# A two-layer graph network on one core: statistics, weight sums, exponentials and adds of the first and last groups in other places

## The chip, the cores and the metric

The kernel runs on one core of a Trainium2 chip. A core has five engines that run side by side: PE (TensorE, matrix products), DVE (VectorE, elementwise work and reductions), ACT (ScalarE, activations and copies), POOL (GpSimd, elementwise work on SBUF) and SP (SyncE, here only a queue for DMA issues). Each engine takes its own instructions strictly in program order and waits on semaphores for the others. The metric is the device time of one execution in microseconds (us).

## The reference

The input x is 128 samples of 128 nodes with 512 features, all float32, and adj a 128 x 128 adjacency matrix. There are two layers, each of the form "normalise, cut at zero, mix, add to x":

```python
h = relu(layernorm(x))                       # layer 0
q, k, v = h @ Wq0.T, h @ Wk0.T, h @ Wv0.T
rel = adj.T * (q @ k.T)                      # per sample, 128 x 128
rel = rel / norm(rel, axis=2)
x = x + rel @ v
h = relu(layernorm(x))                       # layer 1, 8 heads of 64
q, k, v = h @ Wq1 + bq, h @ Wk1 + bk, h @ Wv1 + bv
scores = q @ k.T / 8 + where(adj == 0, -1e9, 0)
x = x + concat_heads(softmax(scores) @ v)
```

## The kernel before

**Groups.** Four samples make a group (G = 4), so there are 32 groups. For every group there is an object of layer 0 and one of layer 1. At any time the kernel has several groups in work: in the order lists, `p` is the group whose layer 1 is being finished, `l` the one in layer 1, `m` the one in layer 0, `n` the layer-1 object of m's group, and `f` the next group, whose input is loaded.

**Products.** A 512 x 512 weight is multiplied with the 512-column activations of a group in the form of Strassen and Winograd with seven half-size products instead of eight. `Product.P1` to `P7` (L244 to L263) are these seven. Each is 8 PE passes of 256 columns (4 matrix instructions, each in two passes). They need sums of quarters of the weight (T1 to T4N, made once by `sums`, L88: four DVE or POOL instructions of 128 x 512) and sums of quarters of the activations (s0 to s3, made per group and layer by `sumA` and `sumB`, L348 and L359: four DVE instructions). Results are gathered with ACT copies (`keep`, L237) and DVE adds (`add`, L241). P6 and P7 and P4 go on in the bank of P1 ("x"), P3 in the bank of P5 ("z"), P2 in one of its own ("y").

**Layer 0.** `stat` (L279) computes mean and variance of a sample on DVE, two instructions; `inv` (L286) makes the reciprocal root and shift on POOL for two samples, four instructions; `hn` (L295) normalises on ACT and sends the result to DRAM, `rd` (L307) issues the reads back on SP, and `T` (L310) finishes the transpose on DVE. For the very first group `hn_pe` and `turn_pe` (L318, L329) transpose on PE instead. Wq0 and Wk0 are folded into one matrix "a" (`weights0`, L117: 16 products into four PSUM banks pa, in the middle of which, after the twelfth, the first half of group 0 is turned). `weights_v0` (L133) turns Wv0 on PE into four banks pwv and makes its sums on POOL. Then `G` is h times a, `R` (L377) the relation, `mask_rel` and `square` (L388, L395) on DVE and ACT, `N` (L399) the norms by a product with ones, `V` the values, and `O`, `xO` (L412, L417) the output and its addition to x.

**Layer 1.** `Q`, `K`, `V` are products; `S` (L438) the scores of one sample into a PSUM tile that exists once; `mk` (L452) adds the mask and takes the negative maxima on DVE; `ex` (L458) is eight exponentials on ACT and a DMA of the result to DRAM; `wr` and `wt` (L470, L473) read it back and transpose it; `A`, `oc`, `rdo`, `ot` (L554 to L579) make the output, turn it through DRAM, scale it and add it to x. The last group has its own ending: `mk_r`, `ex_r`, `tw`, `An`, `fin` (L485 to L528) work without the way through DRAM for its last two samples. `fin` scales on DVE, adds x on POOL, or on DVE for the last sample, and stores by SP.

**Order.** The order of work is written by hand: no scheduler moves anything. Four lists of step names (FIRST, SECOND, ORDER, LAST, L603 to L634) are walked step by step, and each step issues its instructions to its engines, so the order of the names is the order in each engine's queue. FIRST is used for group 0, SECOND for group 1, ORDER for the other thirty, LAST for what is left of layer 1. Before FIRST there is a prologue (L649 to L667): statistics of group 0, loads of group 1 and of layer 1's weights (issued by POOL), normalising of group 0, statistics of group 1, and the weights of layer 0.

**Buffers.** A tile of a pool with n buffers waits until the tile n allocations before it in that pool is no longer read. Of importance here: ps_mm (4 PSUM banks, for all products, pa and pwv), ps_o (2 banks, tag "po"), ps_s (the one score tile), rpool (4 buffers "r": what `keep` copies, a12 and v12 of the weights), and work (2 buffers "o", in the ending).

Of the kernel before, what the change touches and what calls it, by code (L numbers as in the profile page):

```python
# [9 lines left out]
F32 = mybir.dt.float32  # L10
AF = mybir.ActivationFunctionType
ALU = mybir.AluOpType
AX = mybir.AxisListType

P = 128
G = 4
# [5 lines left out]
def kernel(  # L22
# [15 lines left out]
    nc = tc.nc  # L38
# [24 lines left out]
    ps_o = ctx.enter_context(tc.tile_pool(name="ps_o", bufs=2, space=PSUM))  # L63
# [4 lines left out]
    def load(g: int, b: int, queue):  # L68
        xb = xpool.tile([P, D], F32, tag="xb", name=f"xb_{g}_{b}")
        queue.dma_start(xb, x[g * G + b])  # L70
        x_tiles[g, b] = xb


    ident = const.tile([P, P], F32, tag="ident", name="ident")
# [13 lines left out]
    def sums(n: str, w12, eng):  # L88
        c = wc[n]
        eng.tensor_tensor(c[:, T1], w12, c[:, W11], ALU.subtract)  # L90
        eng.tensor_tensor(c[:, T2], c[:, W22], c[:, T1], ALU.subtract)
        eng.tensor_tensor(c[:, T3], c[:, W22], w12, ALU.subtract)
        eng.tensor_tensor(c[:, T4N], c[:, W21], c[:, T2], ALU.subtract)
# [16 lines left out]
    w12 = {}  # L110

    def place(n: str, m: int, ps, w12, copy):

        copy(wc[n][:, W11 if m < 2 else W21, m % 2, :], ps[:, 0:HF])
        copy(w12[:, m, :] if m < 2 else wc[n][:, W22, m % 2, :], ps[:, HF:D])

    def weights0(between):  # L117

        a12 = rpool.tile([P, 2, HF], F32, tag="r", name="a12")
        pa = [ps_mm.tile([P, D], F32, tag="mm", name=f"pa_{m}") for m in range(KD)]  # L120
        for k in range(KD):
            for m in range(KD):
                nc.tensor.matmul(
                    pa[m], lhsT=raw["q"][:, k, ts(m, P)], rhs=raw["k"][:, k, :],
                    start=(k == 0), stop=(k == KD - 1),
                )
            if k == KD - 2:
                between()
        for m in range(KD):
            place("a", m, pa[m], a12, nc.vector.tensor_copy)  # L130
        sums("a", a12, nc.vector)

    def weights_v0():  # L133

        v12 = rpool.tile([P, 2, HF], F32, tag="r", name="v12")
        for m in range(KD):
            pt = ps_mm.tile([P, KD, P], F32, tag="mm", name=f"pwv_{m}")
            for k in range(KD):
                nc.tensor.transpose(pt[:, k, :], raw["v"][:, k, ts(m, P)], ident)
            place("v0", m, pt.rearrange("p k e -> p (k e)"), v12, nc.scalar.copy)  # L140
        sums("v0", v12, nc.gpsimd)
        nc.vector.tensor_scalar(mask, adj_sb, 0.0, NEG, ALU.is_equal, ALU.mult)

    def load1():
        for name, w in (("q", wq1), ("k", wk1), ("v1", wv1)):
            wr = w.rearrange("(k p) d -> p k d", p=P)
            nc.gpsimd.dma_start(
                wc[name][:, W11 : W21 + 1].rearrange("p h k d -> p (h k) d"), wr[:, :, 0:HF]
            )
            nc.gpsimd.dma_start(wc[name][:, W22], wr[:, 2:4, HF:D])  # L150
            w12[name] = wpool.tile([P, 2, HF], F32, tag="wT", name=f"w12_{name}")
            nc.gpsimd.dma_start(w12[name], wr[:, 0:2, HF:D])
        nc.gpsimd.dma_start(bq_sb, bq1.rearrange("(e p) -> p e", p=P))
        nc.gpsimd.dma_start(bk_sb, bk1.rearrange("(e p) -> p e", p=P))
        nc.gpsimd.dma_start(bv_sb, bv1.partition_broadcast(P))

    class Weights1:
        def scale(self):

            SC = HD**-0.5  # L160
            nc.scalar.mul(wc["q"][:, 0:3], wc["q"][:, 0:3], SC)
            nc.scalar.mul(w12["q"], w12["q"], SC)
            nc.scalar.mul(bq_sb, bq_sb, SC)

        def sumq(self):
            sums("q", w12["q"], nc.vector)
# [199 lines left out]
    class Layer0(Layer):  # L366
        n = 0
# [54 lines left out]
    class Layer1(Layer):  # L422
        n = 1
# [104 lines left out]
        def fin(self, b):  # L528
            g, xb = self.g, x_tiles.pop((self.g, b))
            o = work.tile([P, D], F32, tag="o", name=f"o_{g}_{b}")  # L530
            nc.vector.tensor_tensor(
                o.rearrange("p (k r d) -> p k r d", k=NH, r=2),
                self.po.pop(b).rearrange("p (k r d) -> p k r d", k=NH, r=2),
                self.rs.pop(b).rearrange("p (r k) -> p k r", r=2)[:, :, :, None].to_broadcast(
                    [P, NH, 2, HD]
                ),
                ALU.mult,
            )
            (nc.vector if b == G - 1 else nc.gpsimd).tensor_tensor(xb, xb, o, ALU.add)
            nc.sync.dma_start(out[g * G + b], xb)  # L540

        def mkA(self, b):
# [58 lines left out]


    FIRST = """  # L603
        m.sumA m.sumB m.start m.G.P1 f.hn0 f.rd0 m.G.P2 m.G.P5 w.scale m.G.P6 w.sumq m.G.P3 m.V.P1 f.hn1 f.rd1
        w.sumv m.G.P7 m.V.P2 w.sumk m.G.P4 m.V.P5
        m.R m.mask_rel m.square f.T0 m.V.P6 m.V.P3 m.N m.norms m.V.P7 m.O0 m.xO0 m.O1 m.xO1 n.stat0 n.stat1
        n.inv0 m.V.P4 n.hn0 n.rd0 f.T1 m.O2 m.O3 f.sumA f.start f.G.P1 m.xO2 m.xO3 n.stat2 n.stat3 n.inv1
        f.G.P2 f.sumB f.G.P5 n.hn1 n.rd1 f.G.P6 f.G.P3 f.G.P7 n.T0 f.G.P4 n.T1 n.start
    """.split()
    SECOND = """  # L610
# [17 lines left out]
    """.split()  # L628
    LAST = """
        l.Q.P1 p.rdo0 l.sumA l.Q.P2 l.sumB l.K.P1 l.K.P2 p.wt3 l.Q.P5 p.ot0 l.Q.P6 l.Q.P3 l.K.P5 l.K.P6 l.K.P3  # L630
        l.Q.P7 l.S0 l.mk0 l.K.P7 l.Q.P4 l.ex0 l.wr0 l.K.P4 l.S1 l.mk1 p.A1 p.oc1 p.rdo1 l.start_v l.V.P1
        l.ex1 l.V.P2 l.V.P5 l.S2 l.mkA2 l.mkB2 l.V.P6 l.exA2 l.exB2 l.wt0 l.wr1 l.V.P3 l.V.P7 l.S3 l.mkA3 l.mkB3
        l.tw2 l.wt1 l.exA3 l.exB3 l.V.P4 l.An0 l.fin0 l.An1 l.fin1 p.ot1 l.tw3 l.An2 l.fin2 l.An3 l.fin3
    """.split()  # L634
# [1 line left out]
    def run(order, **who):  # L636
        for step in order:
            name, *path = step.split(".")
            at = who.get(name)
            if at is None:  # L640
                continue
            if len(path) == 2:
                getattr(getattr(at, path[0]), path[1])()
            elif path[0][-1].isdigit():
                getattr(at, path[0][:-1])(int(path[0][-1]))
            else:
                getattr(at, path[0])()

    with tc.manual_schedule(engines={EN.PE, EN.SP, EN.Pool, EN.DVE, EN.Activation}):  # L649
        p, l, m = None, None, Layer0(0)  # L650
        for b in range(G):
            m.stat(b)
        m.inv(0)
        m.inv(1)
        for b in range(G):
            load(1, b, nc.gpsimd)
        load1()
        m.hn_pe(0)
        m.hn_pe(1)
        f = Layer0(1)  # L660
        for b in range(G):
            f.stat(b)
        f.inv(0)
        f.inv(1)
        weights0(lambda: m.turn_pe(0))
        m.turn_pe(1)
        weights_v0()  # L667
        for g in range(NG):
            n = Layer1(g)
            if g:  # L670
                f = Layer0(g + 1) if g + 1 < NG else None
            run((FIRST, SECOND, ORDER)[min(g, 2)], p=p, l=l, m=m, n=n, f=f, w=Weights1())
            p, l, m = l, n, f
        run(LAST, p=p, l=l)
# [30 lines left out]
```

## Time and profile before

| | us |
|---|---|
| three runs | 2539.89, 2538.28, 2534.71 |
| median | 2538.28 |
| the profiled execution, its own time | 2538.26 |
| its span, first to last instruction | 2536.5 |

| engine | busy us | share of span | instructions |
|---|---|---|---|
| PE | 2512.7 | 99% | 14672 |
| PE weight loads | 2135.8 | 84% | 14672 |
| DVE | 1707.5 | 67% | 2484 |
| ACT | 1023.9 | 40% | 3248 |
| POOL | 535.0 | 21% | 945 |

The mean granted PE clock is 0.997 of full speed. A line in the order of time gives the start and duration in us, the engine, the line of the kernel, the operation, output and inputs with their shapes, how many instructions are merged in it, and in brackets the idle time of the engine before it with what ended that idle time. A line of waits gives who waited for whom, total us, how often, and the longest.

### The profile page before, as it was taken

The page shows a single profiled execution, that of the slowest core. Times are in us where ns is not written, and L with a number is a line of the kernel's source. Part 1 is how long each engine was busy: PE and PEld are TensorE (multiplying, and loading weights), DVE is VectorE, ACT ScalarE, POOL GpSimd, SP SyncE. Part 2 cuts the span into 40 slices and gives each one's busy share as a digit, 9 for nine tenths or more (in the row PEclk, how much of TensorE's full clock was granted, in tenths as well). Part 3 has the DMA queues.
Part 4 walks back from the last instruction along what each step waited for, and adds up shares of the span by engine and source line. Part 5 has one row for each costly group of instructions (what it writes and reads, how often), then busy time and mean ns, then how long its engine had stood idle before and what let it go on. Part 6 is the DMA issues. An engine that isn't in the chain of part 4 may idle for free.

```text
span 2536.5 us, 40820 instructions
## 1 busy us (share of the span) xinstructions
PE 2512.7 (99%) x14672; PEld 2135.8 (84%) x14672; DVE 1707.5 (67%) x2484; ACT 1023.9 (40%) x3248; POOL 535.0 (21%) x945
## 2 busy tenths in 40 slices
PE   8999999999999999999999999999999999999998
PEld 6888888888888888888888888888888888888886
DVE  5566766667676667666677666676666676666765
ACT  2334443444433344434444333444344443334433
POOL 5121212211122212121111222121211112221211
PEclk9999999999999999999999999999999999999999
DMA  5255544555444555445554445554455644455542
GB/s 171 88 179 166 187 145 140 172 170 185 154 145 151 182 167 183 146 146 168 168 188 152 142 155 178 171 182 142 148 169 165 193 151 143 156 176 174 175 133 93
DMA packets 370475, 405.71 MB, mean 160 GB/s; under 512 B 29600, under 2 KB 286752, under 8 KB 370272
## 3 DMA queue, kind: packets, MB, share of 16 engines
q1 hardware_dynamic: 278992, 167.92, 23.4%
q10 hardware_dynamic: 70384, 166.74, 17.8%
q0 software_dynamic: 20896, 68.44, 7.8%
q8 instruction: 115, 1.88, 0.3%
q14 instruction: 88, 0.72, 0.1%
HBM read 204.80 MB, written 198.18 MB: 159 GB/s over the span
## 4 chain that ended last, share of the span: by engine, by line
PE 97%; DVE 1%; DMA 1%; ACT 0%; issue 0%; POOL 0%; SPq 0%; ACTq 0%; DVEq 0%; POOLq 0%
PE pv_x L218 18%; PE pq_x L218 9%; PE pv_z L218 9%; PE pk_x L218 9%; PE pg_x L218 8%; PE pss L445 5%; PE po L562 5%; PE pv_y L218 5%; PE pg_z L218 4%; PE pq_z L218 4%; PE pr L382 4%; PE pk_z L218 4%; PE po L414 4%; PE pk_y L218 2%; PE pg_y L218 2%; PE pq_y L218 2%
## 5 line engine op out<-in xcount | busy, mean ns | idle before, releaser
L463 ACT ACTIVATE e<-pss,nmax 128x128 f32<-128x128 f32 x1008 | 355.0, 380 | 190.9 <-DVE nmax L456 168.5
L597 POOL TENSOR_TENSOR xb<-xb,o 128x512 f32<-128x512 f32 x124 | 158.2, 1276 | 1103.6 <-DVE o L590 976.4
L218 PE MATMUL pv_x<-wc_v,h 128*128 128x256 f32 x1280 | 300.8, 382 | 0.0
L218 PEld LDWEIGHTS pv_x<-wc_v,h 128*128 128x128 f32 x1280 | 240.3, 190 | 51.0 <-DVE v L242 11.7
L301 ACT ACTIVATE hn<-xb,shift,rstd 128x512 f32<-128x512 f32 x252 | 190.9, 807 | 152.4 <-POOL shift L293 152.4
L218 PE MATMUL pv_z<-wc_v,s 128*128 128x256 f32 x1024 | 245.1, 382 | 0.0
L313 DVE STREAM_TRANSPOSE h<-u_h 128x1024 f32<-128x1024 f32 x126 | 156.5, 1242 | 98.9 <-DMA u_h<-d_h 92.0
L463 ACT ACTIVATION_READ_ACCUMULATOR e<-pss,nmax 128x1 f32 x1008 | 221.2, 219 | 0.0
L454 DVE TENSOR_TENSOR pss<-pss,mask 128x1024 f32<-128x1024 f32 x126 | 154.7, 1228 | 96.2 <-PE pss L445 96.2
L218 PEld LDWEIGHTS pv_z<-wc_v,s 128*128 128x128 f32 x1024 | 192.0, 190 | 28.6
L218 PE MATMUL pv_x<-wc_v,s 128*128 128x256 f32 x768 | 184.9, 384 | 0.0
L218 PE MATMUL pq_x<-h,wc_q 128*128 128x256 f32 x768 | 184.7, 383 | 0.0
L283 DVE BATCH_NORM_STATS2 st<-xb 128x6 f32<-128x512 f32 x256 | 172.0, 672 | 16.6 <-DMA xb<-in_x_dram 16.6
L218 PE MATMUL pk_x<-h,wc_k 128*128 128x256 f32 x768 | 181.5, 379 | 0.0
L445 PEld LDWEIGHTS pss<-kT,qT 64*128 64x128 f32 x2048 | 124.6, 188 | 48.7 <-PE po L414 23.5
L290 POOL TENSOR_SCALAR rstd<-mv 128x2 f32<-128x2 f32 x128 | 28.6, 223 | 642.8 <-DVE mv L284 642.7
L218 PEld LDWEIGHTS pq_x<-h,wc_q 128*128 128x128 f32 x768 | 143.4, 190 | 23.5 <-ACT oT L573 5.1
L218 PEld LDWEIGHTS pk_x<-h,wc_k 128*128 128x128 f32 x768 | 145.8, 190 | 19.9
L218 PEld LDWEIGHTS pv_x<-wc_v,s 128*128 128x128 f32 x768 | 140.8, 190 | 20.4
L456 DVE TENSOR_REDUCE nmax<-pss 128x8 f32<-128x1024 f32 x126 | 154.2, 1224 | 4.4
L478 DVE STREAM_TRANSPOSE wT<-u_w 128x1024 f32<-128x1024 f32 x126 | 150.3, 1193 | 3.6 <-DMA u_w<-d_w 3.6
L445 PE MATMUL pss<-kT,qT 64*128 64x128 f32 x2048 | 149.2, 285 | 2.7 <-ACT e L463 2.3
(147 smaller groups left out, 4460.2 us busy)
## 6 DMA issues: line engine op xcount, KB each, us to landing
d_h<-hn ACTq DMA_DIRECT2D x126, 512.0 KB, 3.5
u_h<-d_h SPq DMA_DIRECT2D x504, 128.0 KB, 3.3
d_w<-e ACTq DMA_DIRECT2D x126, 512.0 KB, 2.6
u_w<-d_w SPq DMA_DIRECT2D x504, 128.0 KB, 2.9
xb<-in_x_dram POOLq DMA_DIRECT2D x124, 256.0 KB, 3.2
d_o<-oT ACTq DMA_DIRECT2D x62, 512.0 KB, 4.1
u_o<-d_o SPq DMA_DIRECT2D x248, 128.0 KB, 3.1
out_dram<-xb POOLq DMA_DIRECT2D x124, 256.0 KB, 2.8
```

What stands on the lines that cost most here:

```text
L218: nc.tensor.matmul(ps[:, m, :], lhsT=lhsT, rhs=rhs, start=first and m == 0 and k == 0, stop=k == 1, skip_group_check=True,)
L283: nc.vector.bn_stats(st, x_tiles[g, b])
L301: nc.scalar.activation(hn[:, r], x_tiles[g, b].rearrange("p (k j q) -> p j k q", j=TB, q=BK), AF.Relu, bias=self.shift[:, b : b + 1], scal ...
L313: nc.vector.transpose(half.rearrange("p k (t i) -> p t k i", i=BK), self.u.pop(i).rearrange("p t (k q) -> p t k q", q=BK),)
L382: nc.tensor.matmul(pr[:, b, :], lhsT=self.turned(k, b), rhs=self.gT[:, k, ts(b, P)], start=(k == 0), stop=(k == KD - 1),)
L445: nc.tensor.matmul(pss[:, r, k, :], lhsT=self.qT[rows, k, ts(b, P)], rhs=self.kT[rows, k, ts(b, P)], start=True, stop=True,)
L454: nc.vector.tensor_tensor(sc, sc, mask[:, None, :].to_broadcast([P, H, P]), ALU.add)
L456: nc.vector.tensor_reduce(self.nmax[b], sc, AX.X, ALU.max, negate=True)
L463: nc.scalar.activation(e[:, :, i, :], sc[:, i, :].rearrange("p (j q) -> p j q", q=BK), AF.Exp, bias=nmax[:, i : i + 1], accum_out=self.tot ...
L478: nc.vector.transpose(self.wT[b].rearrange("p h (t i) -> p t h i", i=BK), self.uw.pop(b).rearrange("p t (h q) -> p t h q", q=BK),)
L562: nc.tensor.matmul(po[r * HD : (r + 1) * HD, k, :], lhsT=self.v[:, b, ts(2 * k + r, HD)], rhs=wT[:, r * NH + k, :], start=True, stop=True,)
L597: nc.gpsimd.tensor_tensor(xb, xb, o.rearrange("p k t q -> p (k t q)"), ALU.add)
```

## The change

Six things are done in other places or in another way; the arithmetic is the same.

1. `weights0` allocates a PSUM tile `warm` in ps_o and lets PE transpose the identity into it eight times before its first product. Nobody reads the tile.
2. `stat` of the four samples of group 1 and both `inv` leave the prologue and go into FIRST: statistics 0 and 1 and `inv0` behind the activation sums of group 0, statistics 2 and 3 and `inv1` behind G.P2.
3. The sums of the weight v0 (POOL) leave `weights_v0` and become the step `w.sumw`, behind f.inv1 in FIRST.
4. `w.sumq` (DVE) moves from ahead of G.P3 to behind V.P2, directly ahead of `w.sumk`.
5. Later in FIRST, m.xO2, m.xO3, n.stat2, n.stat3 and n.inv1 go ahead of f.sumA, f.start and f.G.P1.
6. In LAST, the exponentials of sample 0 (`l.ex0`, `l.wr0`) go ahead of l.Q.P4, and the final add of sample 2 is done by DVE instead of POOL.

On PE eight transposes are added at the head and nothing else changes its order. On ACT, G.P5's copy now precedes f.hn0, and in LAST ex0 precedes the copy of Q.P4. On SP the order is the same, on POOL one instruction is gone.

```diff
@@ -117,6 +117,9 @@
     def weights0(between):
 
         a12 = rpool.tile([P, 2, HF], F32, tag="r", name="a12")
+        warm = ps_o.tile([P, P], F32, tag="po", name="warm")
+        for _ in range(8):
+            nc.tensor.transpose(warm, ident, ident)
         pa = [ps_mm.tile([P, D], F32, tag="mm", name=f"pa_{m}") for m in range(KD)]
         for k in range(KD):
             for m in range(KD):
@@ -138,7 +141,7 @@
             for k in range(KD):
                 nc.tensor.transpose(pt[:, k, :], raw["v"][:, k, ts(m, P)], ident)
             place("v0", m, pt.rearrange("p k e -> p (k e)"), v12, nc.scalar.copy)
-        sums("v0", v12, nc.gpsimd)
+        w12["v0"] = v12
         nc.vector.tensor_scalar(mask, adj_sb, 0.0, NEG, ALU.is_equal, ALU.mult)
 
     def load1():
@@ -161,6 +164,9 @@
             nc.scalar.mul(wc["q"][:, 0:3], wc["q"][:, 0:3], SC)
             nc.scalar.mul(w12["q"], w12["q"], SC)
             nc.scalar.mul(bq_sb, bq_sb, SC)
+
+        def sumw(self):
+            sums("v0", w12["v0"], nc.gpsimd)
 
         def sumq(self):
             sums("q", w12["q"], nc.vector)
@@ -536,7 +542,7 @@
                 ),
                 ALU.mult,
             )
-            (nc.vector if b == G - 1 else nc.gpsimd).tensor_tensor(xb, xb, o, ALU.add)
+            (nc.vector if b >= G - 2 else nc.gpsimd).tensor_tensor(xb, xb, o, ALU.add)
             nc.sync.dma_start(out[g * G + b], xb)
 
         def mkA(self, b):
@@ -601,10 +607,10 @@
 
 
     FIRST = """
-        m.sumA m.sumB m.start m.G.P1 f.hn0 f.rd0 m.G.P2 m.G.P5 w.scale m.G.P6 w.sumq m.G.P3 m.V.P1 f.hn1 f.rd1
-        w.sumv m.G.P7 m.V.P2 w.sumk m.G.P4 m.V.P5
+        m.sumA m.sumB m.start f.stat0 f.stat1 f.inv0 m.G.P1 m.G.P2 f.stat2 f.stat3 f.inv1 w.sumw m.G.P5 f.hn0 f.rd0 m.G.P6
+        w.scale m.G.P3 m.V.P1 f.hn1 f.rd1 w.sumv m.G.P7 m.V.P2 w.sumq w.sumk m.G.P4 m.V.P5
         m.R m.mask_rel m.square f.T0 m.V.P6 m.V.P3 m.N m.norms m.V.P7 m.O0 m.xO0 m.O1 m.xO1 n.stat0 n.stat1
-        n.inv0 m.V.P4 n.hn0 n.rd0 f.T1 m.O2 m.O3 f.sumA f.start f.G.P1 m.xO2 m.xO3 n.stat2 n.stat3 n.inv1
+        n.inv0 m.V.P4 n.hn0 n.rd0 f.T1 m.O2 m.xO2 m.O3 m.xO3 n.stat2 n.stat3 n.inv1 f.sumA f.start f.G.P1
         f.G.P2 f.sumB f.G.P5 n.hn1 n.rd1 f.G.P6 f.G.P3 f.G.P7 n.T0 f.G.P4 n.T1 n.start
     """.split()
     SECOND = """
@@ -628,7 +634,7 @@
     """.split()
     LAST = """
         l.Q.P1 p.rdo0 l.sumA l.Q.P2 l.sumB l.K.P1 l.K.P2 p.wt3 l.Q.P5 p.ot0 l.Q.P6 l.Q.P3 l.K.P5 l.K.P6 l.K.P3
-        l.Q.P7 l.S0 l.mk0 l.K.P7 l.Q.P4 l.ex0 l.wr0 l.K.P4 l.S1 l.mk1 p.A1 p.oc1 p.rdo1 l.start_v l.V.P1
+        l.Q.P7 l.S0 l.mk0 l.K.P7 l.ex0 l.wr0 l.Q.P4 l.K.P4 l.S1 l.mk1 p.A1 p.oc1 p.rdo1 l.start_v l.V.P1
         l.ex1 l.V.P2 l.V.P5 l.S2 l.mkA2 l.mkB2 l.V.P6 l.exA2 l.exB2 l.wt0 l.wr1 l.V.P3 l.V.P7 l.S3 l.mkA3 l.mkB3
         l.tw2 l.wt1 l.exA3 l.exB3 l.V.P4 l.An0 l.fin0 l.An1 l.fin1 p.ot1 l.tw3 l.An2 l.fin2 l.An3 l.fin3
     """.split()
@@ -658,10 +664,6 @@
         m.hn_pe(0)
         m.hn_pe(1)
         f = Layer0(1)
-        for b in range(G):
-            f.stat(b)
-        f.inv(0)
-        f.inv(1)
         weights0(lambda: m.turn_pe(0))
         m.turn_pe(1)
         weights_v0()
```

## The prediction

> **What bounds the kernel now.** I read the page's busy shares first, then TensorE's waits over the whole span, then the order of time in the places that these waits name.
>
> ```profile
> PE 2512.7 (99%) x14672; PEld 2135.8 (84%) x14672; DVE 1707.5 (67%) x2484; ACT 1023.9 (40%) x3248; POOL 535.0 (21%) x945
> ...
> PE pa L123 <- DMA raw_q<-in_L_gnn_Wq_dram: 4.6, 1, 4.6
> PE pwv L139 <- issue: 2.5, 1, 2.5
> PE pss L445 <- ACT e L463: 2.3, 2, 2.0
> PE pg_x L218 <- DVE gT L242: 2.0, 2, 1.2
> PE pq_z L218 <- DVE qT L242: 1.0, 1, 1.0
> ```
>
> TensorE (PE) is busy 99% of 2536.5 us. Asked for 140 to 2480 us alone, its waits are none: thirty groups run with no gap, so what the first groups gain reaches the end undiminished, and only the head and the tail can change the time. All waits together are about 14 us, and the five rows above hold most of them. Now the head, in order of time (start, duration, engine, line; what it idled for is in brackets):
>
> ```profile
> 22.75 0.69 DVE L283 BATCH_NORM_STATS2 st<-xb 128x6 f32<-128x512 f32 x1 [1.21 <-DMA xb<-in_x_dram]
> 23.58 0.66 DVE L283 BATCH_NORM_STATS2 st<-xb 128x6 f32<-128x512 f32 x1
> ...
> 24.38 0.39 DVE L114 COPY wc_a<-pa 128x256 f32<-128x256 f32 x1
> ...
> 25.20 3.31 PE L139 MATMUL pwv<-ident,raw_v 128*128 128x128 f32 x16 [2.53 <-issue]
> ...
> 28.30 2.62 PE L218 MATMUL pg_x<-h,wc_a 128*128 128x256 f32 x8
> ...
> 39.52 1.77 DVE L92 TENSOR_TENSOR wc_q<-wc_q,w_q 128x512 f32<-128x512 f32 x1
> ...
> 44.22 1.99 PE L218 MATMUL pg_x<-h,wc_a 128*128 128x256 f32 x8 [1.22 <-DVE gT L242]
> ```
>
> VectorE (DVE) takes instructions in order. The statistics of group 1 wait there for their x tiles; the copies out of pa stand behind them, start at 24.38, and only they free the banks for pwv. So PE, done at 22.68, idles to 25.20 (named "issue"). The clock pays as well: the granted clock is 0.50 from 26.5 to 29.5 us. That is why the 16 transposes take 3.31 and pg_x 2.62 instead of the usual 1.89. Later P4 of the G product waits for an add that is queued behind the sums of wc_q, each stretched to 1.7 us. The tail:
>
> ```profile
> 2493.40 0.84 ACT L229 ACTIVATE qT<-pq_x,bq_sb 128x256 f32<-128x256 f32 x2 [7.36 <-PE pq_x L218]
> 2494.13 0.37 ACT L463 ACTIVATE e<-pss,nmax 128x128 f32<-128x128 f32 x1
> 2497.09 1.65 PE L445 MATMUL pss<-kT,qT 64*128 64x128 f32 x16 [2.00 <-ACT e L463]
> 2498.67 3.09 PE L562 MATMUL po<-wT,v 128*64 128x128 f32 x32
> ...
> 2526.81 1.27 POOL L597 TENSOR_TENSOR xb<-xb,o 128x512 f32<-128x512 f32 x1
> ...
> 2528.84 1.95 DVE L539 TENSOR_TENSOR xb<-xb,o 128x512 f32<-128x512 f32 x1
> 2528.96 1.27 POOL L539 TENSOR_TENSOR xb<-xb,o 128x512 f32<-128x512 f32 x1
> ```
>
> ScalarE (ACT) waits for the copy of Q.P4 before it may start the exponentials, whose maxima were ready at 2492.24. The second score product needs the bank that they read, so PE idles 2.0 us; then the granted clock is 0.51 from 2497.5 to 2501.0. At the very end the last add takes 1.95 us beside POOL's.
>
> The profiled execution took 2538.26 us (span plus 1.76), practically the shown median of 2538.28; the sum is made against it.
>
> **The change, part by part.** Times in the head are in the old trace's clock, ahead of part (a).
>
> (a) Eight transposes of the identity ahead of the first product. The identity is ready at 1.30 us; a transpose takes 0.109 at full clock (8 in 0.87 in the chain) and 0.196 at half (8 weight loads in 1.57). So they end near 3.1, inside the wait for raw_q until 4.63: cost nothing; were raw_q there first, 1.6. Their use is the clock. From 4.63 to about 9.25 the passes of pa come every 0.855 us, then every 0.43; 24 at 0.43 are 10.3 against 12.86, so 2.5 us are lost to a slow clock. (The clock row shows 1.00 there; I go by durations.) What can be won is capped, because turn_pe(0) follows the twelfth product and needs hn, ready at 15.50 and 16.21, where PE now comes at 17.32: at most 1.4. The Trainium skill, "TensorE: Matmul & The Clock Gate", section "What's actually happening", says that the clock is raised after one busy window of about 3.4 us, sustained, that the windows run free of the kernel's start, and warns not to count on a given number of slow products. Taken literally this gives 0: 1.7 us of transposes fill no window, and a 1.5 us gap follows. The trace is milder. The slow stretch from 26.35 to 29.75 is one such window; the window before it was busy only from 25.20, 33%; the one ahead of 2497.7 about 40%; both lowered the clock, while a 1.2 us gap at 43 (65% busy) didn't. If half full is enough, a random phase gives 0.7 on average (half of the starts win 1.4), if 60% is needed, 0. I take 0.6, ends 0 and 1.4.
>
> (b) f.stat and f.inv leave the place ahead of the products. Eight DVE instructions (4 of 0.66 and 4 of 0.18) no longer stand before the pa copies. Copies m=3 then run from 21.9 to 22.6, pwv starts at 22.7 (raw_v, issued at 4.61 with 9.0 to landing, is there), 16 transposes take 1.9, pg_x 1.73: done at 26.3 instead of 30.9. That is 2.5 of gap and 2.1 of slow clock: **-4.6**. What is late next: DVE now does pa copies to 22.6, sums of a to 25.2, mask, s0 to s3 to 28.05, statistics 0 and 1 to 29.7, P2's add to 30.35, statistics 2 and 3 to 32.05. P5 wants T1 and s0 at 28.05 and has them at 26.0; P2's late add hurts nobody until pv_y at 36.7. On POOL f.inv follows at 29.7 and 32.1 (1.6 each) and the sums of v0 run from 33.7 to 38.8, 4 of 1.27; V.P5 wants the first at 40.15. V.P1's copy needs the r buffer that v12 now holds until the third sum at 37.6, so ACT stands still there from 35.9; behind it are f.hn1 (1.5) and G.P4's copy, wanted by R at 41.9, which comes at 40.8. Slack is about 1 us: cost 0. f.hn0 goes out at 32.9, as before.
>
> (c) sumq behind the three adds. G.P4's wait of 1.22 and its restart vanish (46.21 becomes 44.74 with no other change): **-1.5**. But mask_rel now stands behind sumq and sumk. DVE starts them at 39.1, when POOL starts the sums of v1 (38.8). In the trace such pairs take 1.64 to 1.77 on DVE instead of 0.69 and 1.7 on POOL. POOL's four end near 45.3, so sumq ends at 45.7, sumk (4 of 0.65) at 48.3, rel at 48.95, its squares at 49.65, and N starts at 49.75; PE would be there at 48.9: **+0.85**. Ends: 0 (no stretching: sums done at 44.3, before R's end at 45.45) and +4.6 (all eight stretched).
>
> (d) n.stat2, n.stat3, n.inv1 ahead of f.sumA. Two DVE adds (1.35 together) leave the chain xO3, statistics, hn1, d_h, u_h, T1, qT that ended in PE's 1.02 us wait at 84.83. T1 comes 1.3 earlier: **-1.0**. The d_h transfer in it took 6.17 us, against a median of 3.5, beside x loads, and may not move whole: ends 0 and -1.0. f.P5 wants s0 at 66.98 and gets it at 66.7.
>
> (e) ex0 ahead of Q.P4's copy in LAST. ACT begins at 2492.3, 8 exponentials at a pitch of 0.345 end at 2495.1, just when K.P4 leaves PE (2495.05): **-2.0**, and with no gap the clock stays, so pss takes 1.09 instead of 1.65 and po 1.90 instead of 3.02: **-1.55**. The two P4 copies (0.75 each) end by 2496.8; their values are first read by the third score product.
>
> (f) fin2's add goes from POOL (1.27) to DVE. It starts at 2527.2 beside POOL's add and by the 1.95 row ends at about 2528.7; fin3's product of 0.7 and an add of 0.69 without company follow: 2530.15 instead of 2530.79, **-0.6**. Ends +0.3 and -1.2.
>
> Sum: -0.6 -4.6 -1.5 +0.85 -1.0 -3.55 -0.6 = -11.0; 2538.26 - 11.0 = **2527.3 us**.
>
> **Rivals.** *A third of it is missing*: the queue on DVE is worse (six of its eight sums stretched instead of four or so, N 2.5 late), the transposes win nothing, and d_h is no faster. For it: sums of v0 or v1 that start later on POOL overlap sumk too. Against: POOL's eight ends are counted from rows of this trace. 2527.3 + 1.65 + 0.6 + 1.0 = 2530.5; with all eight stretched and a slow window of clock behind a 4.6 us gap (1.7), 2534.3. *Nothing measurable*: the head's gain is given back because a transfer, such as u_h for T1 or the x loads, sets a later start; only the tail's 4.1 remains: 2534.1, within 0.2%. Against: no transfer ended a PE wait after 4.63; the loads of group 1 landed at 23.5, and the statistics now want them at 28. *Slower*: the new phase of DVE, POOL and the queues costs every one of the 30 groups a wait on PE. It decides from 11.0/30 = 0.37 us a group and shows beyond 0.54; at 0.6 it gives 2545.3. For it: the groups' slack is nowhere shown. Against: their order is unchanged, each starts from PE's own pace, and their waits are zero.
>
> **How the numbers follow.** The forecast 0.72, the smaller gain 0.16, nothing 0.07, slower 0.05. 0.2% is 5.1 us, about what a measurement of this kernel tells from no change (three runs spread over 5.2), so faster means below 2533.2: nearly all of the first two, 0.88; same 0.07; slower 0.05. The bounds of (a) to (f) give 2525 with everything good; the runs' spread adds 1.5 below; upward the range takes in the smaller gain with 2 us of spread and loss: 2523.5 to 2532.5.
>
> **What would show it.** (a) passes of pa at 0.43 from before 9 us. (b) pwv directly behind the second pt, pg_x in 1.89, no granted clock under 1.0 near 27. (c) P4 without a wait, N with one of about 0.9 for sq. (d) pq_z without a wait. (e) the second pss with no gap, po in 1.97. (f) the last add in 0.69. Waits of PE between 140 and 2480 us, or a new one over 2 us in the head, would make the prediction wrong.

## The result, and the profile after

| | us |
|---|---|
| kernel before, 6 runs | 2538.07 median (2534.71 to 2539.89) |
| kernel after, 6 runs | 2528.04 median (2527.08 to 2528.88) |
| ratio | 0.9962, 95% interval 0.9949 to 0.9974 |
| profiled execution after, its own time | 2528.07 |
| its span | 2526.3 |

The change makes the kernel 10.0 us faster; 2527.3 was predicted. The total came out almost as forecast, but two of its terms, (a) and (d), did not, so a part of that is luck.

First the busy shares, then TensorE's waits over the whole span, both after the change (who waited, for whom, total us, how often, longest):

```profile
PE 2510.5 (99%) x14680; PEld 2134.6 (84%) x14680; DVE 1707.7 (68%) x2485; ACT 1023.5 (41%) x3248; POOL 532.8 (21%) x944
```

```profile
PE pq_z L224 <- DVE qT L248: 1.7, 1, 1.7
...
PE pn L408 <- ACT sq L403: 0.4, 1, 0.4
```

The three large waits in the middle of the old list are gone: pwv's 2.5, pss's 2.0 and pg_x's 1.2 for the sums of wc_q. PE's busy time falls by 2.2 us although it has eight instructions more, because fewer of them run at half clock. pq_z, which was to lose its wait, has a longer one: 1.7 instead of 1.0. The wait of group 0's norms for sq is new, 0.4.

The head in order of time (start, duration, engine, line; idle time before it and what ended it in brackets):

```profile
1.35 1.97 PE L122 MATMUL warm<-ident 128*128 128x128 f32 x8 [1.35 <-POOL ident masks.py:199]
4.63 12.70 PE L126 MATMUL pa<-raw_k,raw_q 128*128 128x512 f32 x24 [1.30 <-DMA raw_q<-in_L_gnn_Wq_dram]
...
22.34 1.91 PE L142 MATMUL pwv<-ident,raw_v 128*128 128x128 f32 x16
24.09 1.89 PE L224 MATMUL pg_x<-h,wc_a 128*128 128x256 f32 x8
...
37.90 1.89 PE L224 MATMUL pg_x<-h,wc_a 128*128 128x256 f32 x8
43.38 1.75 DVE L93 TENSOR_TENSOR wc_q<-wc_q 128x512 f32<-128x512 f32 x1
45.05 0.68 DVE L90 TENSOR_TENSOR wc_k<-w_k,wc_k 128x512 f32<-128x512 f32 x1
...
48.98 1.05 PE L408 MATMUL pn<-ones,sq 128*128 128x1 f32 x8 [0.43 <-ACT sq L403]
```

pwv follows PE's work with no gap and takes 1.91 instead of 3.31, pg_x 1.89 instead of 2.62, and G.P4 (37.90) no longer waits. The four sums of wc_q are stretched beside POOL's sums, those of wc_k are not (0.68). The first 24 passes of pa (12 products of two passes each) take about as long as before, 12.70 for 12.86. The middle, where (d) was to work, and the tail:

```profile
63.19 0.59 ACT L232 COPY pg_r<-pg_z 128x512 f32<-128x512 f32 x1 [2.87 <-PE pg_z L224]
63.67 1.52 ACT L307 ACTIVATE hn<-xb,shift,rstd 128x512 f32<-128x512 f32 x2
...
76.32 1.25 DVE L319 STREAM_TRANSPOSE h<-u_h 128x1024 f32<-128x1024 f32 x1 [6.11 <-DMA u_h<-d_h]
...
2489.82 1.16 PE L451 MATMUL pss<-kT,qT 64*128 64x128 f32 x16 [0.21 <-ACT e L469]
2490.91 1.97 PE L568 MATMUL po<-wT,v 128*64 128x128 f32 x32
...
2517.94 1.27 POOL L603 TENSOR_TENSOR xb<-xb,o 128x512 f32<-128x512 f32 x1
2518.31 1.46 DVE L545 TENSOR_TENSOR xb<-xb,o 128x512 f32<-128x512 f32 x1
...
2520.41 0.69 DVE L545 TENSOR_TENSOR xb<-xb,o 128x512 f32<-128x512 f32 x1
```

The second score product has 0.21 of idle time instead of 2.00, takes 1.16 instead of 1.65, and po 1.97 instead of 3.09. The last add ends at 2521.10; before, at 2530.79.

Where the 10.2 us of the two profiled executions come from is read by taking the same PE instruction in both and subtracting its starts; the lead can only change where one of the two waits or runs slowly:

| PE instruction reached | lead us | step of the prediction | predicted | measured |
|---|---|---|---|---|
| first turn of group 0 (pt) | 0.16 | (a) | 0.6 | 0.16 |
| third product of G (pg_y) | 4.93 | (b) | 4.6 | 4.77 |
| after G.P4 (R) | 6.42 | (c), its gain | 1.5 | 1.49 |
| after the norms (V.P7) | 5.72 | (c), its cost | -0.85 | -0.70 |
| Q.P5 of group 0 (pq_z) | 5.15 | (d) | 1.0 | -0.57 |
| LAST | 5.47 | none | 0 | 0.32 |
| last product (pn) | 8.87 | (e) | 3.55 | 3.40 |
| end of the last add | 9.69 | (f) | 0.6 | 0.82 |
| end of span | 10.2 | none | 0 | 0.5 |

Of the 0.32 ahead of LAST, about 0.2 comes from a wait of group 1's norms that only the kernel before has.

### The profile page after: what moved, and what is told of

It reads as the page before. It is cut to its first block, busy times and chain, and to the rows that moved or that the text cites. A ratio compares the mean times of both kernels' runs of the same rounds, so it can differ in the third digit from the quotient of the medians.

```text
span 2526.3 us, 40834 instructions
## 1 busy us (share of the span) xinstructions
PE 2510.5 (99%) x14680; PEld 2134.6 (84%) x14680; DVE 1707.7 (68%) x2485; ACT 1023.5 (41%) x3248; POOL 532.8 (21%) x944
## 4 chain that ended last, share of the span: by engine, by line
PE 96%; DMA 1%; DVE 1%; ACT 1%; issue 0%; POOL 0%; SPq 0%; DVEq 0%; ACTq 0%
PE pv_x L224 18%; PE pq_x L224 9%; PE pv_z L224 9%; PE pk_x L224 9%; PE pg_x L224 8%; PE pss L451 5%; PE po L568 5%; PE pv_y L224 4%; PE pg_z L224 4%; PE pq_z L224 4%; PE pr L388 4%; PE pk_z L224 4%; PE po L420 4%; PE pq_y L224 2%; PE pk_y L224 2%; PE pg_y L224 2%
## 5 line engine op out<-in xcount | busy, mean ns | idle before, releaser
L484 DVE STREAM_TRANSPOSE wT<-u_w 128x1024 f32<-128x1024 f32 x126 | 150.4, 1194 | 3.4 <-DMA u_w<-d_w 3.4
```

Source lines behind the costliest of these rows:

```text
L484: nc.vector.transpose(self.wT[b].rearrange("p h (t i) -> p t h i", i=BK), self.uw.pop(b).rearrange("p t (h q) -> p t h q", q=BK),)
```

## The experiments

The theory was: each step acts by the mechanism that the prediction gave, except (a), which is worth nothing, and (d), which is tied to another queue. The rivals are in the expectations. All diffs are against the kernel after, unless said. Ratios are against runs of the kernel before on the same chip; its medians there were 2537.49 (a0, a16, b_undo, b_undo_fill), 2539.56 (c_undo, d_undo, d_load_sp, e_undo) and 2538.12 (the last four), so differences of about 1 us between kernels of different groups are not read.

### (a): no transposes, and sixteen

```diff
-        warm = ps_o.tile([P, P], F32, tag="po", name="warm")
-        for _ in range(8):
-            nc.tensor.transpose(warm, ident, ident)
```

> The changed kernel without the eight transposes of the identity. Theory A (they never fill a window, so the clock comes up when it would anyway): same as the changed kernel, 2528.0 within 0.6; pa's passes turn from 0.855 to 0.43 us at some point between 8.0 and 11.5 us of the span. Theory B (a window that is half full raises the clock): slower by 0.6 on average, 2528.6.

Measured: 2527.63 us (2526.72 to 2527.95), ratio 0.9962. Without them the kernel is no slower: eight transposes are worth nothing that these runs can tell. In a16, `range(8)` becomes `range(16)`:

> Sixteen transposes instead of eight, so that PE is busy without a gap from 1.35 us to the arrival of raw_q at 4.6. Theory A: the first window that is busy throughout now ends between 4.8 and 8.2 us, so pa's passes turn fast before 8.2 and 3.4 us less are run slowly, worth 1.7, of which the wait for hn (ready at 15.0 and 15.7) leaves about 1.1: 2526.9. Theory B: the same end, since eight had already won most of it in half of the executions: 2527.3. Rival: transposes of this size don't count as activity: 2528.0 and the turn stays near 9 us.

Measured: 2529.15 us (2526.75 to 2532.17), ratio 0.9968 (0.9958 to 0.9979). Two stretches of each profile, passes of pa alone (the stretch, its us, PE's busy time with the number of passes touched, the granted clock, the DMA share, GB/s). The kernel after, then a16, and the whole row of 24 passes in a16:

```profile
4.60:6.60 2.00, 1.97 (x3) 1.00 1.03 397
6.60:8.60 2.00, 2.00 (x4) 1.00 1.06 406
```

```profile
4.60:6.60 2.00, 1.86 (x5) 1.00 1.05 403
6.60:8.60 2.00, 2.00 (x6) 1.00 1.05 405
```

```profile
4.74 10.57 PE L126 MATMUL pa<-raw_k,raw_q 128*128 128x512 f32 x24
```

With sixteen, the passes of this profile come fast from the first or second on, and the row takes 10.57 us instead of 12.70. pwv starts 1.72 earlier. The row is drawn anew in every execution, so one profile would not be enough: in the nine profiles with eight transposes it takes 12.06 to 13.65 us (mean 12.9), in the three without (the kernel before, a0, best0) 12.82 to 13.45 (mean 13.0), in the two with sixteen 10.57 and 11.34. So the clock can be raised ahead of the first product, transposes do count for it, and eight of them do not raise it. The clock column reads 1.00 in both, so it can't be used at the head. The time was not lower, though. In the profile the lead is handed back: G.P7 waits 0.41 for a copy that stands behind f.hn0 on ScalarE, the norms of group 0 wait 0.50, those of group 1 0.76, and Q.P5 of two later groups (at 1773 and 2083 us) loses 0.8 us together.

### (b): the statistics back in front, and the gap filled

b_undo puts `stat` and `inv` of group 1 back into the prologue (the sums of v0 stay where the change put them):

```diff
+        for b in range(G):
+            f.stat(b)
+        f.inv(0)
+        f.inv(1)
         weights0(lambda: m.turn_pe(0))
...
-        m.sumA m.sumB m.start f.stat0 f.stat1 f.inv0 m.G.P1 m.G.P2 f.stat2 f.stat3 f.inv1 w.sumw m.G.P5
+        m.sumA m.sumB m.start m.G.P1 m.G.P2 w.sumw m.G.P5
```

> The changed kernel with group 1's statistics and inv back ahead of the first products (everything else as changed). Theory: PE idles about 2.5 us ahead of pwv again, because pa's copies stand behind statistics that wait for x on DVE, and the granted clock is 0.5 for one window of 3.4 us after it, which costs about 1.9 more: +4.4, 2532.4. Rival (the slow window came from something else, the transfers of that time for example): +2.5, 2530.5, clock at 1.0.

Measured: 2531.32 us (2528.86 to 2532.59), ratio 0.9973. The head in order of time:

```profile
25.30 3.50 PE L142 MATMUL pwv<-ident,raw_v 128*128 128x128 f32 x16 [2.93 <-issue]
28.59 2.13 PE L224 MATMUL pg_x<-h,wc_a 128*128 128x256 f32 x8
```

The gap and the slow products are back, 4.74 us by the end of pg_x against the kernel after. The median is only 3.3 above it (3.7 above a0, on the same chip), since the waits of the norms (0.43) and most of a us at pq_z (0.82 instead of 1.66) vanish when PE comes later: what a step gains at its own place is not what is left at the end.

b_undo_fill keeps PE busy in that gap, to part the idle time from the clock:

```diff
         m.turn_pe(1)
+        fill = ps_o.tile([P, P], F32, tag="po", name="fill")
+        for _ in range(22):
+            nc.tensor.transpose(fill, ident, ident)
         weights_v0()
```

> As the run before, and PE fills the gap with 22 more transposes of the identity (2.4 us) between the turning of h and that of Wv0. Theory (the gap itself lowers the clock): no slow window, pg_x in 1.89, only the gap of 2.5 is left: 2530.5. Rival (the slow window has another cause): pg_x in 2.4 or more, clock 0.5 near 27 us, 2532.4.

Measured: 2534.74 us (2532.41 to 2538.37), ratio 0.9992. The clock half came out: pwv takes 1.91 and pg_x 1.89 at 27.52, so it was the gap that lowered the clock, not the transfers of that time. pg_x comes 1.07 us earlier than in b_undo, although the row of pa took 0.83 longer in this execution. Then group 1 lost more than that. In order of time, and then PE in a stretch behind it (us, PE's busy time, granted clock, DMA share, GB/s):

```profile
116.87 1.05 PE L408 MATMUL pn<-ones,sq 128*128 128x1 f32 x8 [1.62 <-ACT sq L403]
```

```profile
120.00:123.00 3.00, 3.00 (x8) 0.54 0.00 0
```

A wait of 1.62 for the squares was followed by nearly half clock, 0.54. DVE makes `mask_rel` there, and ahead of it in SECOND stands `l.wt0`, which waits for the transfer of the exponentials to and from DRAM. b_fill_late moves only that name, with the filler kept:

```diff
-        l.ex1 l.wr1 l.wt0 m.R m.mask_rel m.square
+        l.ex1 l.wr1 m.R m.mask_rel m.square l.wt0
```

> The kernel with the statistics back in front and 22 filler transposes, now with the transpose of the weights of sample 0 behind the relation of group 1 on DVE. Theory (its 2534.7 came from one late d_w: an instruction packet inside that transfer delays one engine's share by 1.5 us, the transpose waits for it on DVE ahead of the relation, N waits 1.6 us and a slow window of clock follows): N of group 1 without a wait, 3.5 to 4 less, 2530.5. Rival (the filler harms in another way): 2534 and a wait or a slow clock elsewhere.

Measured: 2532.41 us (2530.65 to 2534.69), 2.3 lower. The norms of group 1 no longer wait, and the product behind them runs in 2.00 instead of 3.40: the wait was DVE's queue behind `l.wt0`. It is still 1.9 above the expectation. PE reaches Q.P1 of group 0 0.91 us ahead of b_undo (74.33 and 75.24), but pq_z waits 2.22 instead of 0.82: the second half of u_h is turned at 80.26 and 79.78, so the transfer that (d) speaks of takes the lead away. Another 0.7 us goes in Q.P5 and other places of later groups, each loss too short to be listed as a wait; no run looks into these.

### (c): the sums of wc_q back ahead of G.P3

```diff
-        w.scale m.G.P3 m.V.P1 f.hn1 f.rd1 w.sumv m.G.P7 m.V.P2 w.sumq w.sumk m.G.P4 m.V.P5
+        w.scale w.sumq m.G.P3 m.V.P1 f.hn1 f.rd1 w.sumv m.G.P7 m.V.P2 w.sumk m.G.P4 m.V.P5
```

> The changed kernel with the sums of wc_q back ahead of G.P3's add on DVE. Theory (the parts are not additive: PE now comes 5 us earlier, while the sums still wait for the scaling on ACT, which ends at 35.6): sums from 35.7 to 42.4 beside POOL's, G.P7's add ends near 43.8 instead of 37.1, G.P4 waits 5.5 us, and a slow window of clock follows (1.7); N waits no more (-0.4): +6.5, 2534.5. Rival (additive, as the old trace had it, 1.5 against a wait of 0.85 at N): +0.7, 2528.7.

Measured: 2534.23 us (2532.22 to 2535.09), ratio 0.9979. In order of time:

```profile
43.28 3.78 PE L224 MATMUL pg_x<-h,wc_a 128*128 128x256 f32 x8 [4.58 <-DVE gT L248]
```

G.P4 waits 4.58 us, and the clock halves behind the gap. In the kernel before the same queue cost 1.22. So (b) and (c) are one change: with the statistics moved and sumq left, all of (b)'s gain would be lost in the next wait on the same engine (6.5 us against d_undo, on the same chip).

### (d): the order undone, and the loads taken away

d_undo puts `m.O3 f.sumA f.start f.G.P1` back ahead of `m.xO2 m.xO3 n.stat2 n.stat3 n.inv1`, as before:

> The changed kernel with xO2, xO3, the statistics 2 and 3 of layer 1 and their inv back behind f.sumA and f.G.P1. Theory (hn1 stands behind the copy of f.G.P5 on ACT in either order, so the change won nothing there): pq_z waits 1.0 to 1.2 as in the kernel before, hn1 starts within 0.3 of where it does in the changed kernel against PE, time the same, 2528.0 within 0.6. Rival 1 (the new order costs the 0.65 that the changed kernel's profile shows): 2527.4 and d_h in 6.2. Rival 2 (the new order won its 1.0 and lost it to a transfer): hn1 1.3 later against PE, pq_z waits 2.5 or more, 2529.

Measured: 2527.75 us (2527.46 to 2530.33), ratio 0.9956. Undoing (d) costs nothing that these runs can tell. pq_z waits 1.32 there, less than in the kernel after (1.66), and d_h takes 6.5. hn1 starts at 63.50, right behind the copy of pg_z (62.86), as it does in the kernel after, and as it did in the kernel before:

```profile
68.91 0.59 ACT L226 COPY pg_r<-pg_z 128x512 f32<-128x512 f32 x1 [2.57 <-PE pg_z L218]
69.54 1.52 ACT L301 ACTIVATE hn<-xb,shift,rstd 128x512 f32<-128x512 f32 x2
```

The next run leaves (d) in and moves the loads of group 2 from POOL's queue to SP's, where they stand behind the reads of u_h and leave at 69.31 instead of 63.47:

```diff
-                load(self.g, b, nc.gpsimd)
+                load(self.g, b, nc.sync if self.g == 2 else nc.gpsimd)
```

> The changed kernel with the four x loads of group 2 issued by SP, behind the reads of n.h1, instead of by POOL right after n.inv1. Theory (d_h of hn1 takes 6.9 us because these loads run beside it): d_h in 3 to 4 us, T1 3 us earlier, pq_z without a wait: 1.2 to 1.7 less, 2526.6. Rival (d_h shares the time with the reads of n.h0, not with the loads): d_h near 6, no change, 2528.0. Danger: statistics of group 2 late, which would show as a wait of DVE near 97.

Measured: 2526.18 us (2525.57 to 2526.91), ratio 0.9947 (0.9933 to 0.9962), 1.6 below d_undo on the same chip. The transfers between 60 and 75 us (size of each, median us to landing) of the kernel after, then the same of d_load_sp between 55 and 78, then its second half of u_h in order of time:

```profile
xb<-in_x_dram POOLq DMA_DIRECT2D x4, 256.0 KB, 5.1
d_h<-hn ACTq DMA_DIRECT2D x1, 512.0 KB, 6.9
```

```profile
d_h<-hn ACTq DMA_DIRECT2D x2, 512.0 KB, 2.7
```

```profile
71.63 1.25 DVE L319 STREAM_TRANSPOSE h<-u_h 128x1024 f32<-128x1024 f32 x1 [1.92 <-DMA u_h<-d_h]
```

hn1 starts at 63.17, 0.50 earlier, which is PE's own lead there; but d_h takes 4.2 us less, u_h is turned 4.7 us sooner, and pq_z runs without a wait. The wait that (d) aimed at belongs to the transfer beside the loads. The run moves the loads to another queue and to a later time at once, so it doesn't say which of the two d_h gains by.

### (e) and (f): the tail

e_undo puts `l.Q.P4` back ahead of `l.ex0 l.wr0`:

> The changed kernel with the exponentials of sample 0 of the last group back behind the copy of Q.P4. Theory: the second score product waits 2.0 us, the clock is at 0.5 for 3.4 us after it, pss takes 1.65 and po 3.09 again: +3.4, 2531.4. Rival (the clock doesn't follow the gap): pss 1.16 and po 1.97, +1.9, 2529.9.

Measured: 2529.86 us (2528.13 to 2530.69), ratio 0.9962. In order of time, then PE in the stretch behind (columns as above):

```profile
2492.03 1.16 PE L451 MATMUL pss<-kT,qT 64*128 64x128 f32 x16 [2.00 <-ACT e L469]
```

```profile
2494.00:2497.00 3.00, 3.00 (x29) 1.00 0.37 115
```

The same gap of 2.00 us as in the kernel before, and no slow clock behind it. ScalarE's order makes the gap, as predicted; whether the clock falls too differs between these two profiles.

f_undo gives the add of sample 2 back to POOL (`b >= G - 2` becomes `b == G - 1`):

> The changed kernel with the last add of sample 2 back on POOL. Theory (the two last adds share the way to SBUF): DVE's last add takes 1.95 us instead of 0.69 and ends 0.8 later against PE's last product: +0.8, 2528.8. Rival (the store of another tile ends last): no change, 2528.0.

Measured: 2528.89 us (2528.63 to 2529.70), ratio 0.9961. The last adds of f_undo:

```profile
2520.29 1.95 DVE L545 TENSOR_TENSOR xb<-xb,o 128x512 f32<-128x512 f32 x1
2520.40 1.27 POOL L545 TENSOR_TENSOR xb<-xb,o 128x512 f32<-128x512 f32 x1
```

The two last adds meet again, and DVE's takes 1.95, about its own 0.69 and POOL's 1.27 one after the other. The Trainium skill, "SBUF — State Buffer", section "SBUF: two separate sides", says that an add with two SBUF inputs on VectorE and a GpSimd instruction hold one port pair exclusively, not shared, from start to end, and that the one that starts first has it. The length agrees; the order doesn't, for DVE's record starts 0.11 earlier and it is DVE that is stretched (POOL's records are the rougher ones). In the kernel after, DVE's first add starts when POOL's has 0.90 us left, and takes 1.46, 0.77 more than alone.

### A version below both

From these runs: group 2's loads by SP, `l.wt0` behind `m.square`, `w.sumk` behind f.G.P6 (it is wanted late), G.P6 ahead of f.hn0, f.G.P1 ahead of m.O2, f.sumA behind the statistics, and sixteen transposes (best16) or none (best0). The two lines that were shown above are left out here:

```diff
-        for _ in range(8):
+        for _ in range(16):
...
-        w.sumw m.G.P5 f.hn0 f.rd0 m.G.P6
+        w.sumw m.G.P5 m.G.P6 f.hn0 f.rd0
...
-        m.V.P2 w.sumq w.sumk m.G.P4
+        m.V.P2 w.sumq m.G.P4
...
-        f.T1 m.O2 m.xO2 m.O3 m.xO3 n.stat2 n.stat3 n.inv1 f.sumA f.start f.G.P1
+        f.T1 f.start f.G.P1 m.O2 m.xO2 m.O3 m.xO3 n.stat2 n.stat3 n.inv1 f.sumA
...
-        n.hn1 n.rd1 f.G.P6 f.G.P3
+        n.hn1 n.rd1 f.G.P6 w.sumk f.G.P3
```

> The changed kernel with what the runs point to: sixteen transposes in front; f.hn0 behind G.P6's copy; sumk later, in DVE's idle time ahead of f.G.P3's add; f.G.P1 ahead of m.O2; loads of group 2 by SP; in group 1 the weights' transpose behind the relation. Expected from the waits: -1.7 for the clock at the start, -0.45 at N, -0.7 at O2, -1.9 at pq_z, no loss at N of group 1: 2523.3. If sixteen transposes are worth nothing: 2525.0.

> The run before without any transposes in front. Theory: only the slow clock at the start comes back, +1.7 against the run before, 2525.0. Rival (sixteen transposes are worth nothing, or cost, as the 2529.1 of their first run may mean): the same as the run before or less.

Measured: best16 2525.05 us (2524.33 to 2526.96), ratio 0.9945 (0.9931 to 0.9958); best0 2525.91 us (2524.87 to 2527.29), ratio 0.9949 (0.9936 to 0.9961). best16 is 13.1 us below the kernel before on its chip, and all its runs are below all of the kernel after, taken on another chip. But d_load_sp alone is 13.4 below the kernel before on its own chip, so a gain of the other moves together is not shown. The norms wait for nothing in either profile. What is missing against the expectation is largely one new wait, that I made myself, here in best16:

```profile
59.92 1.99 PE L224 MATMUL pg_z<-s,wc_a 128*128 128x256 f32 x8 [1.30 <-DVE s L362]
```

f.sumA is now queued behind the statistics, and G.P5 of group 1 waits for it. In the profiled executions best16 is 1.97 us ahead of best0 behind pwv, helped by a long row of pa in best0 (13.45), and 1.62 ahead in LAST, where best16 has a new wait of 0.47 behind group 1; the medians show 0.9, and their ranges overlap.

## Why the prediction was right, and where it was wrong

**(a) failed.** The step that fell is "if half full is enough, a random phase gives 0.7 on average". PE was busy from 1.35 to 3.32, less than 2 us, then idle for 1.30; the clock stayed low until about 9 us. The milder reading came from two stretches in which the clock fell (33% and 40% busy) and from one in which it did not (65%), and took it for granted that what keeps the clock up also raises it. The third was misread besides: the gap at 43 us lies across two stretches, 88% and 76% busy. In the traces of the runs a stretch of 3.41 us (counted as in the last section) with 2.81 us of busy time did not raise the clock (b_fill_late, from 4.06 us), one with 3.04 did (d_undo, from 4.05). A stretch with any of the eight transposes in it has at most 2.11, for if products of pa are in it too, so are the 1.30 us of idle time; so eight transposes could not do it at any phase; this is my reading of the traces, not a run of its own. a0 shows that nothing was won, a16 that busy time without a gap wins 2.1 us at the head. The rule of the Trainium skill that was weighed, "TensorE: Matmul & The Clock Gate", section "What's actually happening", one busy window, sustained, gave 0 taken literally, and a0 agrees with that.

**(b) was right in mechanism and size at its place**, 4.77 for 4.6. By the end of the kernel it is worth 3.3 to 3.7 (b_undo), for the reason given there; the sum of the prediction had the norms' part of that cost under (c), and the part at pq_z nowhere.

**(c) was right**: 1.49 for 1.5, and 0.70 for the 0.85 of the norms. sumq's four were stretched and sumk's were not, as worked out. What the prediction did not say is that (c) is what keeps (b): c_undo costs 6.2 us, four times the gain that (c) was given.

**(d) failed**, by 1.57 us. Its step "T1 comes 1.3 earlier" took only DVE out of the chain. On ScalarE, hn1 stands behind f.G.P5's copy, which waits for PE's pg_z; so hn1 keeps its distance from PE, whatever DVE does. It started 5.87 us earlier than in the old profile, where PE's lead was 5.72: 0.15 won, not 1.3. Then d_h took 6.9 us instead of 6.2 beside the loads; what lengthened it by 0.7 is not shown. The lower end of the bound, 0, was still too good: the transfer's length was known to be unusual in the old trace and was not given a range of its own. d_undo and d_load_sp show both halves.

**(e) was right in the gap** (1.80 for 2.0; a wait of 0.21 is left), and its 1.55 us of clock was right for the execution it was computed from (1.60), though the two differences it names, 0.56 and 1.12, make 1.68. e_undo has the gap without the slow clock, so the usual effect of (e) is nearer 2 than 3.5: 1.8 between the profiles of e_undo and of the kernel after, 2.1 between the medians of e_undo and of d_undo, on one chip.

**(f) was right**: 0.6 predicted, 0.82 in the profile, and 0.82 again between f_undo and the kernel after, from the start of PE's last products to the end of the last add (7.56 and 6.74 us). Another 0.5 us lies behind the last add, 5.2 from its end to the end of the span instead of 5.7; f_undo has 5.7 again. So it comes with (f). I take it that the last two stores no longer leave together; no run isolates it.

**The rivals.** Of "a third of it is missing", the parts on the transposes and d_h came true, the part on DVE's sums didn't. (a) and (d) together fell 2.0 us short; gains of 0.3 and 0.5 in places that the prediction left at 0, and small excesses of other terms, gave 1.2 of it back. That the total is off by only 0.7 us is in that part luck. "Nothing measurable" and "slower" fell: no wait of PE appeared in the thirty groups between.

## What to carry to other kernels

Before an instruction is moved forward on one engine, list what stands ahead of its successors on every other engine of the chain, and the transfers at the end; the gain is set by the latest of them, and here ScalarE's order and one slow transfer cancelled DVE's 1.3 us. Cost steps that act on the same engine together: undoing one of two moves cost four times its own term. A slow-clock stretch behind a gap of about 2 us is not a fixed part of the gap's price, so a sum made from one profile should carry it as a range.

## What the runs showed of the hardware

- **The same gap lowers the clock in one execution and not in another.** 2.00 us of idle time ahead of pss gave 0.51 in the kernel before and 1.00 in e_undo. A gap of 1.62 lowered it in b_undo_fill, one of 2.22 (pq_z, b_fill_late) did not. The traces say what differs. In each, the changes of the granted clock lie whole multiples of 3.41 us apart (in the kernel before at 26.35, 29.76 and 2497.60). Count PE's busy time in stretches of that length, laid from a change: the clock fell behind stretches with 1.07 and 1.41 us busy (kernel before), 0.48 (b_undo) and 1.06 (c_undo), and stayed up behind 1.57 and 1.69 (e_undo) and 1.75 (kernel after). The gap ahead of pss lies whole in one stretch in the kernel before and 0.27 us of it outside in e_undo; the 2.22 in b_fill_late are split between two (2.25 and 2.36 busy). b_undo_fill (2.50) fits only if the norms' products of one column each count as idle, and the last 20 us, with their narrower products, do not fit. So this is a reading that no run was made to test.
- **Spread.** The kernel before spreads over 8 us in all its 65 runs (2534.7 to 2542.9), the kernel after over 1.8 in six; its longest wait behind the head is 1.66. That the one follows from the other fits, and was not tested.
- **A 512-KB store to DRAM takes 2.7 us with few neighbours and 6.9 beside four loads of 256 KB issued by POOL.** The store d_h of hn1 takes 6.2 to 7.1 in all eleven kernels with these loads beside it, and 2.7 in the three with the loads on SP's queue, so later.
- **A transfer's tail.** In b_undo_fill the store of exponentials that held `l.wt0` took 4.8 us, against a median of 2.6 for such stores in the kernel after. These rows give the GB/s of 40 equal slices between 100 and 112 us there, and one of the queues that moved something in them (packets, MB, share of the DMA engines):

```profile
GB/s 0 0 0 0 0 0 0 0 0 0 0 0 0 0 0 0 0 0 0 82 464 410 382 355 0 0 14 14 27 14 27 14 0 0 0 0 38 167 260 266
...
q8 instruction: 1, 0.02, 0.9%
```

  After 1.5 us at full rate there is a pause, and then some 20 packets trickle at 14 to 27 GB/s for 1.8 us. One packet of instructions falls inside that transfer. The same is seen in a16, b_fill_late and best16 (4.0 to 5.1 us in the slow store), the other three kernels with more than eight added transposes; in the kernel after, a0, b_undo, d_undo, d_load_sp and e_undo the packet comes at the end of the store or behind it, and the longest of them took 3.3. It is not peculiar to them: each kernel has 126 such stores, and over the fourteen traces 158 of them have such a packet of 16 KB starting in their first 1.5 us. These took 3.2 to 5.1 us, median 3.8; the 1194 with no instruction packet in or just ahead of them have a median of 2.6. So the two go together. That the added instructions move the place at which the next ones are fetched, and that the fetch holds up one DMA engine's share, is my reading; no run moved the fetch alone. If it is so, instructions put into a gap are not free even where the engine is idle, and a part of what a16 and b_undo_fill lost is this.
